# MLP on queries and routing written as one order per engine, with the last group in halves; key scaling moved to VectorE

## The chip, the cores and the metric

The kernel runs on 1 core of one Trainium2 chip. The time is that of the device in microseconds; the value to predict is the median of the runs of the changed kernel. A core has five engines with a queue each, in order: TensorE (PE, with its weight loads PEld), VectorE (DVE), ScalarE (ACT), GpSimd (POOL) and SyncE (SP, which here issues DMAs). They meet through semaphores.

## The reference, cut to what matters

Two layers, each with an attention-like part and a feed-forward part, on 8 x 512 tokens of width 128 in fp32. The change touches the second layer: test-time training (`_L1_attn_ref`) and the routing of the mixture of experts (`_L1_ffn_ref`).

```python
# x: (4096, 128)
q, k, v = split(layernorm(x) @ qkv_w + qkv_b)          # 16 heads of 8
q = q / (norm(q) + 1e-6) * qn_scale + qn_bias          # likewise k
for _ in range(2):                                     # TTT_STEPS
    grads = grad(mean(((swish(k @ gate) * (k @ val)) @ proj - v) ** 2))
    theta = {n: theta[n] - 0.1 * newton_schulz(grads[n]) for n in theta}
x = x + (swish(q @ gate) * (q @ val)) @ proj @ proj_w + proj_b
xt = layernorm(x)                                      # mixture of experts
probs = softmax(xt @ Wg + bg)                          # 8 experts, top 2
gate_vals, exp_idx = top_k(probs, 2)
pos = running count of each token within its expert    # capacity 1229
out = sum over the two experts of gelu(xt @ W1[e] + b1[e]) @ W2[e] + b2[e], weighted
```

The order of counting matters: all first choices come before all second choices.

## The kernel before

The 4096 tokens are 32 tiles of 128, in 8 groups of 4 tiles (`NG`, `G`, `W` = 512 tokens). `x` stays in SBUF throughout. The program runs in stages: the convolution of layer 0 (to about 260 us), its quantised feed-forward (to about 375), the keys (375 to 411), two steps of gradients and Newton-Schulz (411 to 931), the MLP on queries with routing (931 to 1046), scatters until 1058, and the experts.

An object `Line` chains the instructions of an engine in the order in which they are given to it (`vec`, `ten`, `act`). Where no line is used, a scheduler picks the order of the independent instructions.

**Keys** (`ttt`, stage one). For each group: `rows_of` multiplies the turned tokens by the key and value weights into PSUM (`rows`, L1159); `squares` squares on ACT (L1168) and reduces on DVE (`nrm`, L1170); DVE copies the values `v` (L1249); ACT takes the square root (L1253); `over_norm` adds, inverts and multiplies on DVE (L1175 to L1177) into `k`; PE turns `k` (`tp`, L1191); ACT scales the turned keys of the group before into `kt` (`adjusted`, L1196). ACT also copies the turned tokens two groups ahead (L1231) and normalises the group three ahead (L772). POOL applies scale and shift to `k` itself (L1262) and adds the output bias to `x` (L1265). The first gradient products (`pa`, L1489) stand behind the last turn on PE, and ACT loads a function table for the sigmoid behind them (L1493).

**MLP on queries and routing** (`ttt`, last stage, and `Moe.route`). For each group, four chunks of the hidden width: two products into PSUM (`pa` and `pb`, L1308 and L1312; four banks, so two chunks at a time), SiLU on ACT (`sw`, L1316), product on DVE (`ht`, L1317). Then `moe.route` of the group before, 16 output products (`o`, L1323) and the addition to `x` (L1327). No line is used here: the scheduler orders PE, DVE and ACT.

`route` of a group: four turns of `x` on PE (L1667) and their copy `xt`; statistics (L1672, L1673); the inverse root by three Newton steps on DVE (`rsqrt`, L87 to L95); logits on PE (L1679); normalised rows on ACT (L1686); on DVE the choice of two experts (L1692 to L1698), the copy of `hot` for the second (L1699), the row copy for the second (L1707) and running counts over the four tiles (`cum`, `seen`, L1709 to L1713); the count over tokens on PE (`pos`, L1716 and L1717); the places (L1718 to L1728, the last one writes `slot`). At last 8 indirect DMAs from POOL's queue (L1733), four for the second choice and four for the first, one for each tile. Those of the first choice wait for the second-choice DMAs of the group before. `seen` carries the counts from one group to the next.

**Experts** (`Moe.experts`). The load of the first expert's rows (`xe`, L1788, on SP) waits for every scatter. Then turn (L1817), products (L1832), Gelu on ACT (L1835, with its table load), products (L1845) and so on.

Of the kernel before, what the change touches and what calls it, by code (L numbers as in the profile page):

```python
# [1 line left out]

# [5 lines left out]
F32 = mybir.dt.float32  # L8
I32 = mybir.dt.int32
U32 = mybir.dt.uint32  # L10
AF = mybir.ActivationFunctionType
ALU = mybir.AluOpType
# [113 lines left out]
def grp(t, g):  # L126
    return t[:, g * G : (g + 1) * G, :]


def flat(ap):  # L130
    return ap.rearrange("p a b -> p (a b)")
# [780 lines left out]
def fp4_ffn(cx):  # L912
# [7 lines left out]
        "H0 G2 H1 x0 G3 P0 T0 s0 S0 A2 A3 t0 H2 H3 D0 C0 P1 S1 d0 c0 T1 U0 D1 C1 T2 C2 g0 "  # L920
        "R0 R0 W0 K0 U1 f0 O0 u0 a0 f1 f2 W1 g1 K1 W2 K2 a1 W3 E0 K3 f3 K4 K5 K6 R1 K7 R1 "
        "r0 O1 r0 o0 "
# [210 lines left out]
def ttt(cx):  # L1133
# [10 lines left out]
    with ExitStack() as st:  # L1144
# [49 lines left out]
        def adjusted(dst, tp, i):  # L1194

            return nc.scalar.activation(dst, tp, AF.Identity, bias=cols[:, i, 1:2], scale=cols[:, i, 0:1])  # L1196


        with ExitStack() as s1:
# [16 lines left out]
            FIRST, AHEAD = 4, 2  # L1216
# [8 lines left out]
            def normal(g):  # L1225
                normed[g] = xn = p2.tile([P, G, D], F32, tag="xn", name="xn", bufs=3)
                norm.act = act if g > AHEAD else free
                norm.apply(g, xn)
# [11 lines left out]
            for g in range(NG):  # L1240
# [8 lines left out]
                vec(nc.vector.tensor_copy(grp(v, g), cur[:, :, D:]))  # L1249
                if g:  # L1250
                    act(adjusted(kt[:, (g - 1) * W : g * W], tk, 1))
# [4 lines left out]
                over_norm(cur[:, :, :D], root, nrm, grp(k, g), vec)  # L1256
                if g + AHEAD + 1 < NG:
                    normal(g + AHEAD + 1)
                tk = turn(ps, "t", grp(k, g), ten)
# [33 lines left out]
        with ExitStack() as s4:  # L1293
# [10 lines left out]
            for g in range(NG):  # L1304
                ht = p2.tile([P, NF, W], F32, tag="ht", name="ht")
                for c in range(NF):
                    pa = ps_h.tile([P, W], F32, tag="h", name="pa")
                    nc.tensor.matmul(  # L1308
                        pa, gate[:, c * P : (c + 1) * P], qt[:, g * W : (g + 1) * W], start=True, stop=True
                    )  # L1310
                    pb = ps_h.tile([P, W], F32, tag="h", name="pb")
                    nc.tensor.matmul(  # L1312
                        pb, val[:, c * P : (c + 1) * P], qt[:, g * W : (g + 1) * W], start=True, stop=True
                    )
                    sw = p2.tile([P, W], F32, tag="sw", name="sw")
                    nc.scalar.activation(sw, pa, AF.Silu)  # L1316
                    nc.vector.tensor_tensor(ht[:, c, :], pb, sw, ALU.mult)  # L1317
                if g:
                    moe.route(g - 1)
                o = ps_o.tile([P, G, D], F32, tag="o", name="o")  # L1320
                for j in range(G):
                    for c in range(NF):
                        nc.tensor.matmul(  # L1323
                            o[:, j, :], ht[:, c, j * P : (j + 1) * P], w2[:, c, :],
                            start=(c == 0), stop=(c == NF - 1),
                        )
                nc.vector.tensor_tensor(grp(cx.x, g), o, grp(cx.x, g), ALU.add)  # L1327
            moe.route(NG - 1)
# [254 lines left out]

class Moe:
# [67 lines left out]

    def route(self, g):
        cx = self.cx
        nc, tc, p2 = cx.nc, cx.tc, self.p2
        vec = nc.vector

        def small(tag, *shape, dt=F32):
            return p2.tile([P, *shape], dt, tag=tag, name=tag)

        def over_e(t):
            return t.unsqueeze(2).to_broadcast([P, G, E])

        x, at = grp(cx.x, g), slice(g * G, (g + 1) * G)
        tp = self.ps_t.tile([P, G, P], F32, tag="t", name="tp")
        for j in range(G):
            nc.tensor.transpose(tp[:, j, :], x[:, j, :], cx.ident)  # L1667
        xt = small("xt", G, P)
        nc.scalar.copy(xt, tp)
        st, mv = small("st", G, 6), small("mv", G, 2)  # L1670
        for j in range(G):
            vec.bn_stats(st[:, j, :], x[:, j, :])  # L1672
            vec.bn_aggr(mv[:, j, :], st[:, j, :])  # L1673
        rs, off = small("rs", G), small("off", G)
        rsqrt(nc, p2, mv[:, :, 1], 1e-5, rs, G)
        both = self.ps_r.tile([P, 4, G, E], F32, tag="r", name="both")
        pl, pos = both[:, 3], both[:, :3]
        for j in range(G):
            nc.tensor.matmul(pl[:, j, :], xt[:, j, :], self.w_c, start=True, stop=True)  # L1679
        lg = small("lg", G, E)  # L1680
        vec.tensor_tensor(lg, pl, over_e(rs), ALU.mult)
        vec.tensor_tensor(lg, lg, self.b_g.unsqueeze(1).to_broadcast([P, G, E]), ALU.add)
        vec.scalar_tensor_tensor(off, mv[:, :, 0], -1.0, rs, ALU.mult, ALU.mult)
        rows = [self.xr[:, k, at, :] for k in range(K)]
        for j in range(G):
            nc.scalar.activation(  # L1686
                rows[0][:, j, :D], x[:, j, :], AF.Identity, bias=off[:, j : j + 1], scale=rs[:, j : j + 1]
            )

        hot, best, rk, tmp = small("hot", K + 1, G, E), small("best", K, G), small("rk", K, G), small("tmp", G, E)  # L1690
        for k in range(K):
            vec.tensor_reduce(best[:, k, :], lg, AX.X, ALU.max)  # L1692
            vec.tensor_tensor(tmp, lg, over_e(best[:, k, :]), ALU.is_equal)
            vec.tensor_tensor(tmp, tmp, self.rank, ALU.mult)
            vec.tensor_reduce(rk[:, k, :], tmp, AX.X, ALU.max)
            vec.tensor_tensor(hot[:, k], self.rank, over_e(rk[:, k, :]), ALU.is_equal)
            if k + 1 < K:
                vec.scalar_tensor_tensor(flat(lg), flat(hot[:, k]), -1e30, flat(lg), ALU.mult, ALU.add)  # L1698
        vec.tensor_copy(hot[:, K], hot[:, K - 1])  # L1699

        dif = small("dif", G)
        vec.tensor_tensor(dif, best[:, 0, :], best[:, 1, :], ALU.subtract)
        nc.scalar.activation(dif, dif, AF.Tanh, scale=0.5)
        for k, s in enumerate((0.5, -0.5)):
            vec.tensor_scalar(rows[k][:, :, D + 1], dif, s, 0.5, ALU.mult, ALU.add)

        vec.tensor_copy(rows[1][:, :, :D], rows[0][:, :, :D])  # L1707
        cum = small("cum", K + 1, G, E)
        vec.tensor_copy(cum[:, :K, 0, :], self.seen)  # L1709
        for j in range(1, G):  # L1710
            vec.tensor_tensor(cum[:, :K, j, :], cum[:, :K, j - 1, :], hot[:, :K, j - 1, :], ALU.add)
        vec.tensor_tensor(self.seen, cum[:, :K, G - 1, :], hot[:, :K, G - 1, :], ALU.add)
        vec.tensor_tensor(  # L1713
            cum[:, K], cum[:, K - 1], self.seen[:, 0:1, :].to_broadcast([P, G, E]), ALU.add
        )
        nc.tensor.matmul(pos, self.before, hot, start=True, stop=False)  # L1716
        nc.tensor.matmul(pos, self.ones, cum, start=False, stop=True)  # L1717
        vec.tensor_tensor(cum, pos, hot, ALU.mult)  # L1718
        r = small("r", K + 1, G)
        vec.tensor_reduce(r, cum, AX.X, ALU.add)  # L1720
        room = small("room", K, G)
        vec.tensor_scalar(room, r[:, ::2, :], float(CAP), None, ALU.is_lt)

        vec.tensor_scalar(r[:, 1, :], r[:, 1, :], -1.0, CAP - 1.0, ALU.mult, ALU.add)
        vec.scalar_tensor_tensor(flat(rk), flat(rk), -float(PITCH), r[:, :K, :].rearrange("p k g -> p (k g)"), ALU.mult, ALU.add)
        vec.tensor_tensor(rk, rk, room, ALU.mult)
        slot = small("slot", K, G, dt=I32)
        vec.tensor_scalar(slot, rk, float(R), None, ALU.add)  # L1728

        new = []  # L1730
        for k in (1, 0):
            for j in range(G):
                sc = nc.gpsimd.indirect_dma_start(  # L1733
                    out=self.slots.rows[:, :],
                    out_offset=bass.IndirectOffsetOnAxis(ap=slot[:, k, j : j + 1], axis=0),
                    in_=rows[k][:, j, :], in_offset=None, bounds_check=self.limit, oob_is_err=False,
                )
                tc.declare_no_dep(sc.ins, group="scatter", reason="order kept below")
                tc.add_to_no_dep_group("scatter", sc.ins)
                if k == 0 and g:  # L1740
                    self.after(sc, self.scatters[-1][:G])
                new.append(sc.ins.name)
        self.scatters.append(new)
# [178 lines left out]
```

## Time and profile before

| | us |
|---|---|
| median of 3 runs | 1241.97 (1241.28 to 1242.0) |
| profiled execution | 1242.23 |
| its span | 1240.5 |
| PE busy | 1098.0 (89%) |
| DVE busy | 754.1 (61%) |
| ACT busy | 488.5 (39%) |
| POOL busy | 736.9 (59%) |

The profiled execution is 1.7 longer than its span; what lies around the span does not show in the trace. In the views, an entry is: start, duration, engine, line of the kernel, operation, output <- inputs, and in brackets the idle time of the engine before it with what ended that. A group of matmuls (x8) counts passes: an fp32 product of two operands is two passes, a turn is one.

### The profile page before, as it was taken

What the parts mean: (1) busy time and instruction counts of PE and PEld (TensorE: products, weight loads), DVE (VectorE), ACT (ScalarE), POOL (GpSimd) and SP (SyncE); (2) the same over time, 40 slices, a digit from 0 to 9 for tenths busy, and PEclk for the clock granted to TensorE, in tenths of its full rate; (3) what the DMA queues carried; (4) which work ended last, traced back from release to release, by engine and by line L of the source; (5) the groups of instructions that cost most, each with busy time, mean ns of one, the idle gap of its engine ahead of it and who ended that gap; (6) DMA issues with size and microseconds to landing.
All of it is one profiled execution on the core that took longest, in us unless ns stands there. A gap on an engine that the chain in (4) does not pass through costs nothing.

```text
span 1240.5 us, 15616 instructions
## 1 busy us (share of the span) xinstructions
PE 1098.0 (89%) x5343; PEld 664.7 (54%) x5343; DVE 754.1 (61%) x1791; ACT 488.5 (39%) x1005; POOL 736.9 (59%) x720
## 2 busy tenths in 40 slices
PE   6899997848987799999988999999899994799983
PEld 4343442436666455555566555555576663578773
DVE  6899999988986544444455444444466785123364
ACT  4656554435657322222244232222343331243331
POOL 1356666735656888888822888888500666255552
PEclk9999999889999999999999999999999996799997
DMA  5323435960000000000000000000000111221256
GB/s 155 90 81 111 130 91 178 338 184 13 1 1 1 1 1 1 1 0 1 1 1 1 1 1 0 1 1 1 1 1 1 44 44 43 61 70 52 66 195 207
DMA packets 54606, 67.27 MB, mean 54 GB/s; under 512 B 6927, under 2 KB 32350, under 8 KB 54528
## 3 DMA queue, kind: packets, MB, share of 16 engines
q1 hardware_dynamic: 48544, 56.57, 14.7%
q0 software_dynamic: 4608, 8.43, 2.1%
q10 hardware_dynamic: 1376, 1.29, 0.3%
q8 instruction: 42, 0.69, 0.2%
q14 instruction: 36, 0.29, 0.1%
HBM read 40.00 MB, written 27.13 MB: 54 GB/s over the span
## 4 chain that ended last, share of the span: by engine, by line
PE 59%; DVE 22%; ACT 9%; issue 4%; DMA 3%; POOL 3%; ACTq 0%; DVEq 0%; POOLq 0%; SPq 0%
PE ph L1537 5%; PE po L1845 5%; PE sum L1512 5%; PE pp L1527 4%; PE ph L1832 4%; PE sum L1511 4%; PE sum L1513 4%; PE pa L1489 4%; PE pb L1491 4%; DVE v L858 3%; PE cv L492 2%; DVE pr L483 2%; PE pt L1520 2%; PE eg L357 1%; DVE ht L1317 1%
## 5 line engine op out<-in xcount | busy, mean ns | idle before, releaser
L1502 POOL TENSOR_TENSOR ds<-sw,s 128x512 f32<-128x512 f32 x64 | 81.6, 1276 | 86.3 <-DVE sw L1497 86.3
L1504 POOL TENSOR_TENSOR ds<-ds,s 128x512 f32<-128x512 f32 x64 | 111.7, 1745 | 5.0
L1733 POOL DMA_INDIRECT rows<-xr,slot x64 | 62.9, 983 | 73.8 <-DVE rs L95 45.1
L1495 ACT COPY b<-pb 128x512 f32<-128x512 f32 x64 | 37.5, 586 | 162.1 <-PE pb L1491 161.5
L1859 POOL DMA_INDIRECT res<-ye,xe x60 | 58.5, 974 | 66.9 <-DVE ye L1857 28.1
L472 POOL TENSOR_TENSOR pr<-base,en 128x512 f32<-128x512 f32 x52 | 75.0, 1473 | 36.8 <-ACT en L428 36.5
L1835 ACT ACTIVATE ht<-ph,b 128x512 f32<-128x512 f32 (+2 forms) x104 | 56.7, 576 | 94.0 <-PE ph L1832 92.7
L1499 DVE TENSOR_TENSOR h<-sw,b 128x512 f32<-128x512 f32 x64 | 50.2, 785 | 70.6 <-ACT b L1495 70.3
L483 DVE TENSOR_TENSOR pr<-base,w 128x3072 f32<-128x3072 f32 (+2 forms) x27 | 86.3, 3206 | 0.8 <-ACT w L426 0.8
L1503 POOL TENSOR_TENSOR ds<-sw,ds 128x512 f32<-128x512 f32 x64 | 82.8, 1294 | 5.0
L1505 POOL TENSOR_TENSOR ds<-ds,b 128x512 f32<-128x512 f32 x64 | 81.6, 1274 | 5.0
L1527 PEld LDWEIGHTS pp<-proj,ht 128*128 128x128 f32 x512 | 67.1, 191 | 30.7 <-issue 29.8
L1845 PE MATMUL po<-w,ht 128*128 128x128 f32 (+1 forms) x640 | 78.1, 279 | 0.0
L1522 ACT COPY ht<-pt 128x512 f32<-128x512 f32 x64 | 37.6, 587 | 101.5 <-PE pt L1520 101.5
L1832 PE MATMUL ph<-xt,w 128*128 128x512 f32 (+2 forms) x208 | 73.9, 500 | 4.0 <-DVE xt L1820 4.0
L1497 DVE TENSOR_TENSOR sw<-pa,s 128x512 f32<-128x512 f32 x64 | 44.3, 691 | 53.7 <-ACT s L1493 53.7
L1845 PEld LDWEIGHTS po<-w,ht 128*128 128x128 f32 (+1 forms) x640 | 74.9, 190 | 0.6
L1539 DVE TENSOR_TENSOR db<-ph,sw 128x512 f32<-128x512 f32 x64 | 44.2, 691 | 47.2 <-PE ph L1537 47.2
L1537 PE MATMUL ph<-proj_t,dpt 128*128 128x512 f32 x128 | 71.6, 641 | 0.0
L492 PE MATMUL cv<-pr,sel 128*32 128x512 f32 x512 | 62.3, 616 | 8.6 <-DVE pr L483 8.6
L1489 PE MATMUL pa<-gate,kt 128*128 128x512 f32 x128 | 66.8, 604 | 3.4 <-ACT b L1495 3.3
L1512 PE MATMUL sum<-db,k 128*128 128x512 f32 x128 | 66.2, 598 | 1.6 <-DVE db L1539 1.6
(359 smaller groups left out, 2548.4 us busy)
## 6 DMA issues: line engine op xcount, KB each, us to landing
base<-far SPq DMA_DIRECT2D x64, 268.0 KB, 5.2
rows<-empty SPq DMA_DIRECT2D x1, 5005.0 KB
res<-zero SPq DMA_DIRECT2D x1, 4096.0 KB, 27.1
own<-zero SPq DMA_DIRECT2D x2, 2048.0 KB, 18.8
w<-in_L_ffn_W SPq DMA_DIRECT2D x16, 256.0 KB, 4.9
y<-res SPq DMA_DIRECT2D x16, 256.0 KB, 5.5
xe<-rows SPq DMA_DIRECT2D x7, 585.0 KB, 4.3
y<-own SPq DMA_DIRECT2D x12, 256.0 KB, 5.4
```

The source lines that it names most:

```text
L483: vec(nc.vector.tensor_tensor(s["pr"][g][:, lo:hi, :], s["base"][:, lo:hi, at], w.to_broadcast([P, hi - lo, L]), ALU.mult))
L492: ten(nc.tensor.matmul(s["cv"][32 * j : 32 * (j + 1), :], sel[:, i].rearrange("p a h -> p (a h)"), s["pr"][g][:, i * NJ + j, :], start=(g ...
L1489: nc.tensor.matmul(pa, ki, gate, start=True, stop=True)
L1502: nc.gpsimd.tensor_tensor(ds, sw, s, ALU.mult)
L1503: nc.gpsimd.tensor_tensor(ds, sw, ds, ALU.subtract)
L1504: nc.gpsimd.tensor_tensor(ds, ds, s, ALU.add)
L1505: nc.gpsimd.tensor_tensor(ds, ds, b, ALU.mult)
L1512: nc.tensor.matmul(sums[1], ki, db, **kw)
L1527: nc.tensor.matmul(pp, ht[:, c * P : (c + 1) * P], proj[:, c, :], start=(c == 0), stop=(c == NF - 1))
L1537: nc.tensor.matmul(ph, dpt, proj_t, start=True, stop=True)
L1832: ten(nc.tensor.matmul(ph[:, :n], self.w1[:, e, c * P : (c + 1) * P], xt[:, :n], start=True, stop=True))
L1845: ten(nc.tensor.matmul(po[:m, i - lo, :], ht[:, c, (i - lo) * P : (i - lo) * P + m], self.w2[:, e, c, :], start=(c == 0), stop=(c == NF - ...
```

## The change

*Keys.* The scaling of the turned keys goes from ACT to DVE (all groups but the last), the value copy stands behind the key product instead of ahead of the root, and 12 products of the identity with itself stand on PE ahead of the turn of the last group.

*MLP and routing.* `Moe.route` becomes a class `Route` with the same steps as generators that put their instructions on lines. Each group runs through a table of names (`ORDER`, for the last one `LAST`): a letter for a step and a number (of a chunk, a tile or a count of instructions). `H`, `S`, `G`: hidden products, SiLU, gated product of a chunk; `O`, `x`: output products of a tile, addition; `h`, `s`: first chunk of the next group. Of the group before: `t`, `u` turn and its copy; `a` statistics; `b` roots (14 instructions); `l` logits; `c`, `d` first and second choice; `n`, `m` rows and row copy (now on ACT); `e` counts; `v` the count over tokens; `f` places and scatters. In `LAST` the capital letters T, U, A to F, L, M, N and V are the routing of the last part itself.

The last group is cut into two halves of two tiles, each with its own MLP and routing. On ACT instead of DVE: the copy of `hot`, the row copy and the gate weights. The scatters of the first choice no longer wait one by one: a small memset on POOL waits for the second-choice scatters of the group before, and they stand behind it. Behind everything ACT runs one Gelu of a single column.

```diff
+                if g:
+                    vec(nc.vector.tensor_scalar(
+                        kt[:, (g - 1) * W : g * W], tk, cols[:, 1, 0:1], cols[:, 1, 1:2], ALU.mult, ALU.add
+                    ))
-                vec(nc.vector.tensor_copy(grp(v, g), cur[:, :, D:]))
-                if g:
-                    act(adjusted(kt[:, (g - 1) * W : g * W], tk, 1))
                 root = ps_n.tile([P, G, H], F32, tag="n", name="root")
                 act(nc.scalar.activation(root, nrm, AF.Sqrt))
...
                 over_norm(cur[:, :, :D], root, nrm, grp(k, g), vec)
+                vec(nc.vector.tensor_copy(grp(v, g), cur[:, :, D:]))
...
+                if g == NG - 1:
+                    busy = ps.tile([P, W], F32, tag="t", name="busy")
+                    for _ in range(BUSY):
+                        ten(nc.tensor.matmul(busy[:, :P], cx.ident, cx.ident, start=True, stop=True))
                 tk = turn(ps, "t", grp(k, g), ten)
...
-            for g in range(NG):
-                ht = p2.tile([P, NF, W], F32, tag="ht", name="ht")
...
-                if g:
-                    moe.route(g - 1)
...
-            moe.route(NG - 1)
+            ORDER = (
+                "a2 t0 a4 H1 u0 a2 S1 l0 b1 G0 b8 H2 S2 b4 G1 b1 H3 n0 S3 n1 n2 n3 m0 c7 G2 c1 d4 G3 O0 "
+                "O1 d3 e6 v0 O2 O3 f6 x0 f2 h0 s0 "
+            )
+            LAST = (
+                "a1 H1 S1 t0 u0 a6 G0 H2 S2 a1 l0 b9 b4 G1 b1 H3 c1 S3 n0 n1 G2 c1 n2 n3 m0 G3 c2 O0 O1 "
+                "c4 d1 x0 T0 U0 d1 A1 d1 A1 d1 A2 d3 L0 e1 B1 e1 B1 e1 B1 e3 v0 B5 f1 B2 f1 B1 f1 B1 f1 "
+                "B1 f1 B1 N0 N1 C1 f1 C1 f2 C1 M0 C5 D7 E4 V0 F8 "
+            )
+            vec, ten, act = Line(tc), Line(tc), Line(tc)
+            parts = [(g * G, G) for g in range(NG - 1)] + [(NT - G, G // 2), (NT - G // 2, G // 2)]
...
+            ahead = wp.tile([P, 1], F32, tag="ahead", name="ahead")
+            act(nc.scalar.activation(ahead, cx.eps[1e-5], AF.Gelu_apprx_tanh))
...
+class Route:
...
+    def spread(self):
+        self.act(self.moe.cx.nc.scalar.copy(self.rows[1][:, :, :D], self.rows[0][:, :, :D]))
...
+    def second(self):
...
+        yield from self.choose(1)
+        self.act(nc.scalar.copy(self.hot[:, K], self.hot[:, K - 1]))
+        yield self.vec(nc.vector.tensor_tensor(dif, self.best[:, 0, :], self.best[:, 1, :], ALU.subtract))
+        self.act(nc.scalar.activation(dif, dif, AF.Tanh, scale=0.5))
+        for k, s in enumerate((0.5, -0.5)):
+            self.act(nc.scalar.activation(self.rows[k][:, :, D + 1], dif, AF.Copy, bias=0.5, scale=s))
...
+    def places(self):
...
+        for k in (1, 0):
+            if k == 0 and lo:
+                gate = nc.gpsimd.memset(self.small("gate", 1), 0.0)
+                m.after(gate, m.scatters[-1][: len(m.scatters[-1]) // K])
+            for j in range(n):
+                sc = nc.gpsimd.indirect_dma_start(
...
```

## The prediction

> **What bounds the kernel now.** The page comes first: TensorE (PE) is busy for 89% of the span, but that is an average. The windows by stage show where it is not the limit. Columns: stretch, its length, busy time of PE, weight loads, VectorE (DVE), ScalarE (ACT) and GpSimd (POOL), granted clock, DMA share, GB/s.
>
> ```profile
> 1008.00:1021.00 13.00, 12.40 (x63) 8.22 (x63) 10.25 (x59) 4.64 (x10) 7.71 (x9) 1.00 0.12 42
> 1034.00:1046.00 12.00, 4.67 (x20) 3.63 (x19) 9.43 (x66) 2.44 (x6) 7.57 (x9) 0.56 0.14 45
> 1046.00:1062.00 16.00, 0.00 (x0) 0.00 (x0) 0.00 (x0) 0.00 (x0) 9.14 (x10) 0.50 0.22 65
> ```
>
> The first is one group of the MLP on queries with routing, PE and DVE both nearly full. In the other two the last routing runs alone, then POOL alone issues scatters. The timeline there:
>
> ```profile
> 1019.89 0.68 DVE L1327 TENSOR_TENSOR x<-o,x 128x512 f32<-128x512 f32 x1
> ...
> 1033.10 0.68 DVE L1327 TENSOR_TENSOR x<-o,x 128x512 f32<-128x512 f32 x1
> ...
> 1037.16 0.17 DVE L1728 TENSOR_SCALAR slot<-rk 128x8 int32<-128x8 f32 x1 [0.24 <-DVE sq L93]
> ...
> 1037.61 0.97 POOL L1733 DMA_INDIRECT rows<-xr,slot  x1 [2.29 <-DVE rs L95]
> ...
> 1045.79 0.17 DVE L1728 TENSOR_SCALAR slot<-rk 128x8 int32<-128x8 f32 x1 [0.18 <-DVE rk L1726]
> ...
> 1056.92 0.97 POOL L1733 DMA_INDIRECT rows<-xr,slot  x1 [0.30 <-issue]
> 1059.35 0.93 SPq L1788 DMA_DIRECT2D xe<-rows  x2
> ```
>
> The slots of group 6 are there at 1037.3, 4.1 us after the add of group 7; from then POOL issues 16 scatters at 1.28 us each without a gap, and the experts' first load follows the last one's start by 2.43. The last slots (1046.0) come before POOL is free for them (1047.97). So the end of this stage is: slots of group 6, plus 16 scatters. Only an earlier start of those 16 moves it.
>
> The chain of waits at the end of the keys:
>
> ```profile
> 407.32 0.70 DVE k L1177
> 408.02 0.14 issue
> 408.15 1.09 PE tp L1191 x4
> 409.24 1.72 PE pa L1489 x2
> 410.96 0.03 ACTq L1493
> 410.99 0.03 issue
> 411.02 1.28 ACT L1493
> ```
>
> Four transposes that take 0.64 at 404.88 take 1.09 here, and a product pair that elsewhere takes 0.86 takes 1.72: the window 407.45 to 410.85 has a granted clock of 0.50, after PE had idled from 405.5 to 408.15.
>
> **Keys.** Inside the loop the period is 3.52 (square at 391.08, 394.60, 398.11). ACT alone fills it: square 0.64, key scaling 0.70, root 0.16, copy of the turn 0.48, four normalisations 1.54, start to start. Without the scaling ACT's next root must wait for DVE's reduction of the square: square 0.62, reduction 0.70, hand-over 0.02, then 0.16, 0.48, 1.54: 3.52 again. DVE's own list (0.60 reduction, 0.60 scaling, 0.24, 0.59, 0.61, 0.60 value copy) is 3.24. The loop's period gains nothing; ACT's freed time becomes a wait.
> At the head, the value copy moves behind the key product, so k of group 0 is ready 0.47 earlier (382.2 becomes 381.7) and the products `rows` of group 2 start about 0.75 earlier; they run at half clock until 387.45 now and hold the next square. I take -0.9; ends 0 and -1.2 (ACT is next late then).
> At the tail, DVE gets 0.60 more per group and the last k is ready at 407.2 instead of 407.3: -0.1. The 12 idle products are 24 passes (L1301: eight for four products) of 0.11, 2.6 us, issued after the turn of group 6 (405.5): they end at 408.1, when the last k is there; if they run late, the cost is at most 0.2. With full clock the turn saves 0.45 and the first product pair 0.86: -1.3. The last value copy now ends at 408.5 and frees the PSUM that the first product takes; that is when the turn ends, so nothing. Keys in all: **-2.3**, between -1.0 and -2.8. The gradients behind are bound by PE (445.9 of 460 us busy) and only shift.
> The Trainium skill ("TensorE: Matmul & The Clock Gate", Part 1) speaks against the idle products: it says that the clock falls after an idle window of about 3.4 us. The gap here is 2.65, and the clock fell all the same; by the rule the 1.3 would be nothing, by the row it stands.
>
> **One full group of the MLP with routing.** In the new order DVE does the routing of the group before as one chain. Cadences from rows of before (start to start): dependent operations of 128x4 0.197, of 128x32 0.2245.
>
> ```profile
> 947.17 0.16 DVE L94 TENSOR_TENSOR sq<-sq,half 128x4 f32<-128x4 f32 x1
> 947.37 0.16 DVE L95 SCALAR_TENSOR_TENSOR rs<-sq,rs 128x4 f32<-128x4 f32 x1
> 947.56 0.16 DVE L93 TENSOR_TENSOR sq<-rs 128x4 f32<-128x4 f32 x1
> 947.62 0.19 PEld L1312 LDWEIGHTS pb<-qt,val 128*128 128x128 f32 x1 [0.24 <-DVE rs L95]
> 947.64 0.69 DVE L1317 TENSOR_TENSOR ht<-pb,sw 128x512 f32<-128x512 f32 x1
> ```
>
> The next of the chain starts at 948.25: a gated product set between two links costs 0.69 - 0.20 = 0.49. From the start of one add `x`: add 0.71; statistics 1.18 (L742 to L754 at 376.10 to 377.28); 14 links of the roots 2.7; 12 links to the second `hot` 2.69; four gated products 1.96; `dif`, `cum`, `seen` 1.38 (0.22 each at 1042.40 to 1043.50). Sum 10.6. Then PE: prefix products and hand-over 0.25, output products O2 and O3 (16 passes, 0.1115 each, and 0.2 to land) 2.0. The next add starts after **12.85**. Places (1.25 us on DVE) lie beside O2 and O3; DVE waits there for about 1 us in all.
> Others: PE's list is 8 x 0.86 + 0.43 + 0.92 + 3.57 + 0.40 = 12.2, the floor. ACT gets the row copy, the hot copy and the gate weights (about 1.2 us) and sums to 6: free. Hidden H3 ends 8.0 after the add, before its gated product at 8.6; the copy of `hot` on ACT is done at 10.1, before the prefix needs it. POOL: 8 x 1.28 and one gate, a small memset (L338: 0.12), 0.3 with its hand-over: 10.5, below 12.85.
> Before, the adds are 13.03 apart (954.94 to 1033.10, six periods). The periods themselves grow from 12.7 to 13.2, which I can't explain from the lists; so the bounds are 12.4 and 13.4.
> The Trainium skill ("SBUF — State Buffer", the "DVE blocks DMA" trap) says that POOL can't write descriptors while DVE copies SBUF to SBUF in fp32. The scatters under such a row copy (L1707, 0.43) took 1.04, 1.05 and 1.11 instead of 0.97, so moving it to ACT is worth 0.1 a group on POOL by the rows, and 0.4 by the rule.
>
> **Start and halves.** The first add comes at 942.4 instead of 943.1: the 0.86 pair of group 1 no longer stands ahead of the output products (939.46 + 2.92). Six periods on, the add of group 6 is at 942.4 + 77.1 = 1019.5, where before has 1019.9: nothing gained up to here. Then the first half: its gated products are half as wide (0.37 for 128x205, L1820), so each costs 0.18, not 0.49; `cum` is done at 9.4, prefix 0.45, places 1.1, add at 10.95, slots of group 6 right behind it, POOL at 11.5: **1031.0 instead of 1037.6**, because slots come 0.3 after an add, not 4.1, and the add itself is 2 us nearer. POOL's own queue is free by then (1020.4 + 10.5 = 1030.9).
> From there: 15 x 1.28 + 3 gates of 0.3 to the last start, 1051.1, load at 1053.5 instead of 1059.35: **-5.85**. The halves must keep up: first half, 40 links of 0.1 to 0.22 with interleaving, slots 11.1 after its add (1041.5; POOL arrives at 1041.5); second half 16.3 (1046.8; POOL arrives at 1046.9). It just fits.
> **Clock in the tail.** PE idles some 2.5 us before the half-width gated product, and before fell to 0.50 at 1035.5 with such gaps. Each half-clock window adds up to 1.1 to the slots of group 6 and, over the last half (O0, O1, T, L, V at twice their time), up to 3 to the last slots. I take +1.0; ends 0 and 3.9.
> The early table load for Gelu: now 1.28 at 1066.52, but the products beside it run until 1070.5 at half clock, and PE takes up the output at 1070.9 either way. 0, at best -0.2; if those products were at full clock it would be worth 1.28.
>
> **Sum.** -2.3 - 5.85 + 1.0 = -7.15. The profiled execution took 1242.23 (span 1240.5 and 1.7 around it), 0.26 over the median of 1241.97: 1235.1 by the profile, **1234.8** as a median.
>
> **Rivals.**
> 1. *Slower: the strict chain.* DVE now waits in line at every gated product and every join; before, two routings were interleaved on it, at 0.08 to 0.12 between starts (959.59, 959.67, 959.74), which hid such waits. Each 0.1 us lost in a group is paid 7 times. From a period of 14.0 on, gain and loss cancel (7.15 / 6.5 = 1.1 over 12.85); at 14.3 the time is 1244. For it: PE's list leaves only 0.65 us of slack. Against: every producer in the list above is ready 0.5 us or more before its taker.
> 2. *Cold tail.* Both halves at half clock throughout: -1.9 instead of -4.85 in the tail; 1237.8.
> 3. *Gates stall POOL.* Each waits for the landing of scatters (2.3 to 3.6 us). If each stood 2.4 us, POOL would need 12.6 a group and be the bound from the slots of group 0 (955.9): 63 x 1.28 + 8 x 2.4 to the last start, 1055.7, -1.2 in the tail; 1238.5. Against: a gate waits for scatters of the group before, issued over 10 us earlier (5 us for the last).
> 4. *Not what it says:* the VectorE scaling frees no ACT time that counts; that is in the sum already.
>
> **Chances.** Forecast 0.58, cold tail 0.15, gates 0.07, strict chain 0.20 (a quarter of it within the limit of 0.2%, 2.5 us, which is about what a measurement tells from no change). Of the first three 0.76 end faster, 0.04 within. Faster 0.76, same 0.09, slower 0.15. Range: low end a period of 12.5, no half clock, keys at -2.8 (-2.3 - 1.0 - 0.5): 1231.0. High end 13.2 from the third group on (+2), cold tail (+2.9), keys at -1.0 (+1.3): 1241.0.
>
> **What would show it.** Adds 12.85 apart; group 6's first scatter 6.6 us earlier relative to the first add; POOL's last 16 scatters without a gap; the first product of the gradients at 0.86 a pair. A period of 13.5 or more, or a gap of POOL among the last 16, proves me wrong.

## The result, and the profile after

| | before | after |
|---|---|---|
| median of 20 runs each | 1241.53 (1240.57 to 1245.02) | 1238.89 (1235.54 to 1241.69) |
| ratio after / before | | 0.9972, 95% interval 0.9965 to 0.998 |
| profiled execution | 1242.23 (span 1240.5) | 1237.22 (span 1235.3) |
| a later set (e5), median | 1243.02 | 1237.14; ratio 0.9961, 0.9948 to 0.9974 |

By the ratios the change is faster by 3.5 us (second set: 4.8), by the medians by 2.6 (5.9), where 7.15 was forecast. The time is in the range and on the forecast side; the size is about half. The runs fell on several chips; on those of e1 to e4 and of f1 to f4 the kernel before takes 1275 us, which is told there.

The windows that were shown of before, now of after (same columns):

```profile
1008.00:1021.00 13.00, 12.48 (x70) 8.86 (x69) 10.79 (x55) 5.57 (x15) 7.88 (x9) 1.00 0.13 42
1034.00:1046.00 12.00, 5.04 (x30) 3.80 (x28) 10.64 (x73) 4.55 (x17) 8.43 (x10) 0.90 0.14 45
1046.00:1062.00 16.00, 3.81 (x10) 2.24 (x10) 1.85 (x8) 1.26 (x2) 5.94 (x7) 0.50 0.38 109
```

The full group looks as before: PE nearly full. The last routing (second line) fills DVE, and POOL is busy through it at 8.43 instead of 7.57. The timeline of after at the same place:

```profile
1019.73 0.69 DVE L1356 TENSOR_TENSOR x<-o,x 128x512 f32<-128x512 f32 x1 [0.52 <-PE o L1348]
...
1031.04 0.42 DVE L1356 TENSOR_TENSOR x<-o,x 128x256 f32<-128x256 f32 x1
1031.37 0.16 DVE L1789 TENSOR_SCALAR slot<-rk 128x8 int32<-128x8 f32 x1
...
1032.29 0.97 POOL L1797 DMA_INDIRECT rows<-xr,slot  x1 [1.01 <-DVE mv L1687]
...
1043.60 0.97 POOL L1797 DMA_INDIRECT rows<-xr,slot  x1 [1.29 <-DVE rk L1732]
...
1052.61 0.97 POOL L1797 DMA_INDIRECT rows<-xr,slot  x1 [0.30 <-DMA rows<-xr,slot]
1055.04 0.93 SPq L1922 DMA_DIRECT2D xe<-rows  x2
```

Group 6's slots come 0.33 after the first half's add, and its first scatter starts at 1032.29 instead of 1037.61. Counted from the first add that is 91.28 us where before has 94.52. The first half's scatters find POOL waiting (1.29 instead of 0.30). The load follows the last start by 2.43, as before: 4.31 earlier.

The chain of waits at the end of the keys:

```profile
404.23 0.63 PE tp L1191 x4
404.86 2.68 PE busy L1264 x24
407.54 0.05 issue
407.59 0.63 PE tp L1191 x4
408.22 1.03 PE pa L1552 x2
```

No half clock: the turn takes 0.63 (1.09 before), the first product 1.03 (1.72). The idle products hold the turn by 0.1: it starts 3.36 behind the turn before it, and 3.26 in e3, which has none.

Executions of one kernel start the keys at different times, since the code ahead, which the change leaves alone, loses clock in changing places: the first product of the keys starts at 360.97 in before's profiled execution, at 361.38 in after's, at 363.00 in e5's. The traces are therefore compared by stretches, each from one event of the timeline to the next (us):

| stretch | forecast | before | after | e5 (after again) | e6 | e7 | e8 |
|---|---|---|---|---|---|---|---|
| first product of the keys to last gradient product | -2.3 | 532.12 | 530.03 | 530.00 | 530.02 | 530.01 | 529.98 |
| to the first add | -0.7 | 50.00 | 49.60 | 49.59 | 50.86 | 49.60 | 50.86 |
| six more adds | +0.3 | 76.80 | 78.72 | 78.71 | 75.07 | 78.73 | 74.84 |
| add of group 6 to the last scatter's start | -5.4 | 37.03 | 32.88 | 32.86 | 33.49 | 32.79 | 33.41 |
| to the experts' first turn | 0 | 5.45 | 5.23 | 5.34 | 5.31 | 5.37 | 5.36 |
| to their first output product | 0 | 8.53 | 8.04 | 7.96 | 8.85 | 5.54 | 7.17 |
| to the end | 0 | 169.62 | 169.44 | 168.97 | 169.03 | 169.35 | 168.33 |
| sum | -8.1 (+1.0 for clock) | 879.55 | 873.94 | 873.43 | 872.63 | 871.39 | 869.95 |

From the keys on, after is 5.6 us shorter in this pair (6.1 with e5). The gain is in the keys (2.1), at the first add (0.4), between the add of group 6 and the last scatter (4.15) and behind it (0.9). Over the six groups between, the new lines are 1.9 us *slower* than the scheduler's order.

### The profile page after: what moved, and what is told of

Same layout as the page of the kernel before. It is cut to its first block, busy times and chain, and to the rows that moved or that the text cites. A ratio compares the mean times of both kernels' runs of the same rounds, so it can differ in the third digit from the quotient of the medians.

```text
span 1235.3 us, 15732 instructions
## 1 busy us (share of the span) xinstructions
PE 1098.2 (89%) x5387; PEld 666.7 (54%) x5387; DVE 767.0 (62%) x1808; ACT 493.4 (40%) x1041; POOL 737.2 (60%) x728
## 3 DMA queue, kind: packets, MB, share of 16 engines
q0 software_dynamic: 4608, 8.43, 2.1%
q10 hardware_dynamic: 1376, 1.29, 0.3%
## 4 chain that ended last, share of the span: by engine, by line
PE 60%; DVE 21%; ACT 9%; issue 4%; DMA 3%; POOL 3%; ACTq 0%; DVEq 0%; SPq 0%; POOLq 0%
PE ph L1600 5%; PE sum L1575 5%; PE pp L1590 4%; PE sum L1574 4%; PE sum L1576 4%; PE po L1979 4%; PE pa L1552 4%; PE ph L1966 4%; PE pb L1554 4%; DVE v L859 3%; PE cv L493 2%; DVE pr L484 2%; PE pt L1583 2%; PE o L1348 2%; DVE ht L1341 1%
```

## Experiments

**The kernel again** (e5: no edit).

> The changed kernel itself, beside before and the three variants of this set: -3.5 us against before (ratio 0.9972). In the set ahead of this one the chip gave before 1275 us and TensorE's completions reached the other engines 2 to 4.5 us late in the routing stage; if this chip does so too, the changed kernel is 20 us or more faster than before, if not, 3 to 4.

1237.14 (1235.78 to 1240.74), ratio 0.9961 (0.9948 to 0.9974). The two sets agree within their intervals, and the table shows every stretch of e5 within 0.5 us of after's. The mechanism repeats. Of the 5 us spread of single executions part lies ahead of these stretches: the two traces start the keys 1.6 us apart.

**Keys alone** (e1: before plus the keys part), **the rest alone** (e2), **no idle products** (e3).

```diff
 e1: before's queries and routing; keys as changed
 e2: -  vec(tensor_scalar(kt[g-1], tk, scale, bias))      +  act(adjusted(kt[g-1], tk, 1))
     -  12 idle products;  value copy back ahead of the scaling
 e3: -  if g == NG - 1: 12 idle products
```

> The kernel before with the keys part alone (key columns scaled by VectorE, values copied after the over-norm, twelve idle products ahead of the last turn); queries and routing as before. The forecast's sum gives -2.3 us against before (head 0.9, 0.1 at the last k, 1.3 from a warm clock). The trace of the whole change reads -1.7, since the idle products end 0.1 after the last keys and the scaling on VectorE took 0.80 us: if that reading is right, -1.7 here, between -1.3 and -2.0. If the warm clock gave nothing it would be -0.9.

> The changed kernel with the keys part of before: only queries, routing and the halved last group are new. The forecast's sum gives -4.85 us for this part. The two profiled executions read -3.3 (5.0 less 1.7), the medians of the two kernels about -1 to -1.8. If the part is worth what the sum says, -4.85; if the group period is 13.05 and not 12.85 and the last half waits for its own choices, -3.3; if most executions also lose clock in the tail that the profiled one kept, -1 to -2, with a spread of some us between executions.

> The changed kernel without the twelve idle products. TensorE is then idle for about 2.7 us ahead of the last turn of the keys. By the row of before (a gap of 2.65 us, and the turn and the first two products at half clock) it is 1.2 to 1.4 us slower than the changed kernel, with the granted clock at 0.5 for one window about 407 us. If a gap this short left the clock alone, it would be 0.1 us faster, for the idle products end 0.1 us after the keys are ready.

On their chip before took 1275.12 (1271.81 to 1277.82), e1 1273.3 (ratio 0.9988, 0.9977 to 0.9999), e2 1254.31 (0.984, 0.9823 to 0.9858), e3 1252.07 (0.9821, 0.9805 to 0.9836). The 20 us of e2 and e3 belong to the routing on this chip (below) and test none of the sums. Up to the routing the traces are those of any chip, and there they decide. The ends of the keys, timeline of PE, first e2 (keys as in before):

```profile
409.06 0.63 PE L1191 MATMUL tp<-ident,k 128*128 128x128 f32 x4 [2.65 <-DVE k L1177]
409.52 1.02 PE L1546 MATMUL pa<-gate,kt 128*128 128x512 f32 x2
410.38 1.02 PE L1548 MATMUL pb<-val,kt 128*128 128x512 f32 x2
```

then e3 (keys as changed, no idle products):

```profile
409.12 0.66 PE L1191 MATMUL tp<-ident,k 128*128 128x128 f32 x4 [2.64 <-DVE k L1177]
409.77 1.65 PE L1548 MATMUL pa<-gate,kt 128*128 128x512 f32 x2
411.21 1.92 PE L1550 MATMUL pb<-val,kt 128*128 128x512 f32 x2
```

The same gap, 2.65 and 2.64: e2 keeps the full clock, e3 loses it at 410.2. So a gap of this length costs the clock in some executions and not in others. The half clock comes and goes in steps of 3.41 us. In the step that ends with e3's loss (406.77 to 410.18) TensorE was busy for 1.06 us; in e2 the gap falls into two such steps, with 1.82 and 1.44 us busy (403.67 to 407.09 to 410.50). In e3 the loss costs 0.56 at the last gradient product (530.56 from the first product of the keys, against 530.00), not the 1.2 to 1.4 expected: the pair ends 1.4 later, but the pipeline behind it takes up most. And e2, before's keys at full clock throughout, needs 529.79, which is 0.24 *less* than the changed keys. The 2.1 us of the table are then before's two lost windows (383.5 and 407.5), not its work.

What the change does is to make such a loss less likely. With idle products ahead of the last turn, none of eleven traces loses a window there; f4 (below) is one of them, and its keys, otherwise those of before, take 530.55. Without them two of three do (before and e3, not e2). At the head, TensorE waits 2.19 us for the first turn of `k` in before's order and 1.79 in the changed one. None of the eleven traces with the changed order loses a window there; of the three with before's order two do (before, with 1.22 us busy in that window, and f4, with 1.39), and e2, with 1.67, does not. e1's keys take 530.05, and its median says -1.8 with an interval of -0.1 to -2.9, which fits; in what share of its executions before loses these windows, the runs don't show.

**The last group whole** (e4; f2 the same with the idle products of e7).

```diff
-  parts = 7 groups + two halves;  LAST interleaves both halves' routing
+  parts = 8 groups;  LAST = "ORDER, then T0 U0 A8 L0 B9 B5 N0..N3 C7 M0 C1 D7 E6 V0 F8"
```

> The changed kernel with the last group whole: eight full groups, its route alone at the end. By the rows of after its add falls at 1032.8 (1019.73 + 13.05), its slots 11.1 later at 1043.9 or, with the clock lost, 1044.9, and POOL then has eight scatters of 1.28 us and a gate ahead: last start at about 1054 to 1055 and not 1052.6. So 1.5 to 2.5 us slower than the changed kernel. If POOL's queue alone set the end, as the forecast has it (16 scatters back to back from 1032.3), halves would bring nothing: 0.

> The kernel of e7 with the last group whole. Its add falls at about 1033.0 (1019.9 + 13.1), its slots 10 to 11 us later; the eight scatters behind it start at 1044 to 1045, the last at 1053.5 to 1055 against 1052.7 of e7. So 1 to 2 us slower than e7 (ratio to before 0.9948). If POOL's queue alone sets the end, halves bring nothing, and this is within 0.5 us of e7.

Both fell on the other kind of chip. e4 took 1248.23, 3.8 *less* than e3 beside it, which differs by the halves and by the idle products (0.56). First add to last scatter is 120.90 in e4 and 124.06 in e3. f2 took 1252.45 beside 1253.65 for f3, which has the halves and lacks the early table load; first add to last scatter is 123.91 in f2 and 123.64 in f3. f2's idle products ended at 1063.02, 9.67 ahead of the turn, so its tail was cold all the same (turn 1.09, first products 6.04). There the halves are no gain, against the expectation; what they are worth where before takes 1242 us was not run, and stays open: the 4.15 of the table are read from traces, and no run on such a chip separates the halves from the new order.

**Another order of the tables** (e6).

```diff
-  a2 t0 a4 H1 u0 a2 S1 l0 b1 G0 b8 H2 S2 b4 G1 b1 H3 n0 S3 ... c7 G2 c1 d4 G3 O0 O1 d3 e6 v0 O2 O3 f6 x0 f2 h0 s0
+  H1 S1 a2 t0 u0 a6 H2 S2 b3 G1 l0 H3 b9 b2 n0 S3 ... c4 G2 h0 s0 c4 G3 O0 O1 O2 d7 e6 v0 g0 O3 f3 x0 f5
   # and: LAST without its G0; the gated product of the very first chunk ahead of all groups
```

> The changed kernel with another ORDER: the gated products 1 to 3 earlier in VectorE's line, the first hidden products of the next group ahead of the last output products, its first gated product in the wait for the prefix, and the add between the third and the fourth of the steps behind the prefix. If the period is set by VectorE's line with its two waits (0.52 and 0.62 to 0.65 us) on TensorE, both waits are filled and TensorE's own work (about 12.5 us a group) is next: a period of 12.5 against 13.05, some 3 us off the changed kernel. If the waits only move (TensorE already within 0.5 us of its own bound, with ScalarE's Silu between two products), the period stays within 0.15 of 13.05 and the time within 1 us.

The period falls to 12.51 on average (12.22 to 12.66; six adds 75.07 instead of 78.72), as the first theory says. DVE's line of after, and then of e6, at the prefix and the add:

```profile
991.87 0.26 DVE L1782 TENSOR_TENSOR cum<-pos,hot 128x96 f32<-128x96 f32 x1 [0.65 <-PE pos L1776]
993.62 0.69 DVE L1356 TENSOR_TENSOR x<-o,x 128x512 f32<-128x512 f32 x1 [0.52 <-PE o L1348]
```

```profile
991.12 0.26 DVE L1783 TENSOR_TENSOR cum<-pos,hot 128x96 f32<-128x96 f32 x1
991.98 0.69 DVE L1356 TENSOR_TENSOR x<-o,x 128x512 f32<-128x512 f32 x1
```

Both waits are gone. But the time is 1238.51 (1233.97 to 1240.85; ratio 0.9966, 0.9951 to 0.9981), no better than e5 beside it. The table says where the 3.6 us went: 1.26 back at the first add (the next group's products stand ahead of its output products), 0.6 in the last halves, 0.9 in the experts' first products, whose half clock ran longer. Only 0.8 is left from the keys on (873.43 to 872.63).

**Idle products in the tail** (e7), **and with e6's order** (e8).

```diff
-  ... E4 V0 F8
+  ... E4 W0 V0 W1 F8      # W: 16, then 44 idle products into a free bank
```

> The changed kernel with idle products on TensorE in the tail: 16 ahead of the last half's sums, 44 behind them, into a free bank. If the half clock in the tail is what costs, the last half's sums come 0.5 us earlier, the experts' first turn takes 0.6 and not 1.09 us and their first eight products 3.4 and not 5.74: 2.8 us off the profiled execution, more off the median, and a smaller spread between executions than the 6 us of the changed kernel. If the clock comes back late whatever is done (the last idle product ends some us ahead of the first expert's rows), nothing: within 0.5 us.

> The order of e6 and the idle products of e7 together. If they act on different stretches the gains add: about 6 us off the changed kernel. If POOL's queue of scatters is next once the slots come earlier (eight scatters a group take 10.5 us, so it isn't within a period of 12.5), the sum falls short by what POOL waits less.

e7: 1235.86 (1234.9 to 1236.34), ratio 0.9948 (0.9935 to 0.9961); the spread is 1.4 us where e5 has 5.0. PE's timeline of after at the experts' start, and then of e7:

```profile
1057.84 1.09 PE L1951 MATMUL tp<-ident,xe 128*128 128x128 f32 x4 [11.25 <-DMA xe<-rows]
1059.86 5.74 PE L1966 MATMUL ph<-xt,w 128*128 128x512 f32 x8 [0.94 <-DVE xt L1954]
```

```profile
1046.38 10.06 PE L1378 MATMUL busy<-ident 128*128 128x128 f32 x88
1058.10 0.63 PE L1956 MATMUL tp<-ident,xe 128*128 128x128 f32 x4 [1.67 <-DMA xe<-rows]
1059.67 3.70 PE L1971 MATMUL ph<-xt,w 128*128 128x512 f32 x8 [0.94 <-DVE xt L1959]
```

The stretch falls from 8.04 to 5.54; all others stay within 0.15. By the medians e7 is only 1.3 under e5 beside it. The sums of the last half are read 0.24 us sooner behind their input (0.5 was expected), but the last scatter does not move (32.79 against 32.88), because POOL is the later of the two there. e8: 1234.63 (1233.31 to 1235.2), ratio 0.9938 (0.9925 to 0.9951), the best of all runs: 2.5 under e5's median beside it, 8.4 under before's. From the keys on e8 is 3.48 shorter than e5, where e6 alone has 0.80 and e7 alone 2.04: the gains add, but not to the 6 that was expected. The late first add and the slower halves of e6 stay, and the tail gave less than in e7: e8's idle products ended at 1054.2, 1.7 us ahead of the turn as in e7, but here the clock fell for one window at 1057.3, and the first products took 5.33. TensorE was busy for 0.91 us in the 3.41 ahead of that, where e7's last idle products ran until 1056.4 and its windows (1053.97 to 1060.80) have 2.47 and 1.76.

**Mending e8** (f1: the first group in the old order of products, the first half in after's order, 50 idle products, four more behind the first turn), **the price of the early table load** (f3: e7 without `ahead`), **before with idle products alone** (f4).

```diff
 f1: +  {0: START, 1: SECOND, NG - 1: HALF, NG: LAST}.get(i, ORDER)    W: 16, 50;  4 behind the first turn
 f3: -  act(activation(ahead, eps, Gelu))
 f4: before + 12 idle products ahead of the last turn of the keys, 62 behind the last sums
```

> The order of e6, with the first group in the old order of products (its add came 1.26 us late in e6), the first half in the changed kernel's own order, and idle products in the tail as in e7, six more of them, and four behind the experts' first turn. By the rows of e8: the first add back to 941.2 from 942.3, the period 12.5, no half clock in the experts' first products (5.33 to 3.7 us). So 2 to 3 us under e8 (ratio to before 0.9938), near 1232, with a spread of 2 us. If the first interval only gives back what the first add gains, 1 to 1.5 us under e8, from the clock alone.

> The kernel of e7 without the early activation that brings in Gelu's table. The load (1.28 us) then stands ahead of the experts' first Gelu. With the clock at full the eight first products take 3.7 us and the four Gelus behind the load end 0.4 to 1.3 us later: that much slower than e7. If the load still fits beside the products, as at half clock in before, 0.

> The kernel before, with its schedule as it was, and idle products in two places: the twelve ahead of the last turn of the keys, and 62 behind the last group's sums, up to the experts' first turn. If the clock alone explains much of the change, this is 3 to 5 us faster than before: 0.5 to 2 in the keys (before loses the clock there in some executions and in others not) and 2.5 to 3 at the experts' first products. Then the lines of queries and routing are worth the rest of e7's 6 us, 1 to 3. If the clock matters little, within 1 us of before.

All three fell on a chip of the other kind (before 1275.15, 1271.6 to 1278.54), so their times say nothing on e8: f1 1254.07 (ratio 0.9833), f3 1253.65 (0.9834), f4 1275.69 (1.0008, 0.9996 to 1.002). What their traces show: f1's first add is back at 49.60 and its experts' first stretch at 5.54, both as meant. But on that chip the idle products end late, at 1077.2 in f1 and 1076.0 in f3, and hold up the experts' first turn: from the last scatter to it are 7.08 and 7.78, where e3 has 5.48. Of the 2.65 that the first products gain on e3's 8.19, that gives back 1.6 and 2.3. Whether f1 beats e8 where before takes 1242 us is open. f4 gains nothing as a whole. Its keys are 1.57 shorter than before's (530.55 against 532.12), but its other idle products do not stand where they were meant to. No line holds them: they run from 1058.3 on, and 72 of their 124 passes stand ahead of the last sums. The last prefix is read 5.2 us behind its products, POOL waits 3.68 for the slots, and the last scatter starts 46.66 behind the add of group 6, where e1 has 42.82. They ended at 1086.5, 9.3 us ahead of a turn that came at 1095.77 here, so the tail was cold again. What the clock alone is worth in the tail of before stays open. f3 shows the table load, timeline of ACT:

```profile
1079.08 1.28 ACT L1972 ACT_TABLE_LOAD   x1 [17.39 <-PE ph L1969]
1080.37 2.42 ACT L1972 ACTIVATE ht<-ph,b 128x512 f32<-128x512 f32 x4
```

In e7 the Gelus wait for their products; here they run back to back behind the load and catch up with PE. The output products start 5.54 behind the turn in both and take 4.23 instead of 3.74: at full clock the preload is worth 0.5.

## Why the prediction was half right

By its own steps, in the frame of the table; the forecast said -7.15, the pair of profiled executions measured -5.6, and the medians -2.6 (ratio: -3.5). Of its own signs of being wrong one came true, the gap of POOL among its last 16 scatters, and the period is over 12.85 though not at 13.5; the first scatter of group 6 is 3.2 us earlier relative to the first add, not 6.6 (by the forecast's own times, 942.4 and 1031.0, it would be 5.9).

- *Keys, -2.3:* measured -2.1 in the pair, and that it is so near is luck: the price was read off an execution of before that had lost two windows, as part of its schedule. e2, with before's keys and no loss, leaves nothing to gain. "The loop's period gains nothing" came out: squares are 3.51 to 3.52 apart in after (383.20 to 397.27), as in e2. The -0.9 at the head is the lost window at 383.5: the turn of group 6's keys starts 43.91 behind the first product of the keys in before, 42.85 in after, 42.84 in e2. At the tail DVE is slower than assumed: the scaling takes 0.72 from start to start and not 0.60, DVE is busy for 16.38 of 17.00 us (387 to 404), and the last two turns come 3.44 and 3.36 apart, in e2 3.28 and 3.27.
- *First add, -0.7:* -0.4; the 26 passes behind the last gated product take 3.17 until the last one ends, not 2.92.
- *Period 12.85:* 13.12 over the six. Between the adds at 993.62 and 1006.67 the chain to the end of `cum` takes 10.68 (forecast 10.6), the prefix's round on PE to O2 0.36 (0.25), O2 and O3 with their landing 2.01 (2.0): 13.05. Two of the six are longer: 13.34, where a gated product waits on PE (0.24 at 987.63), which the list gave 0.5 us of room, and 13.19, from small delays along the chain. This is the mis-sized term, +1.6 over six groups. e6 takes O2 out of that path and reaches 12.51, so the chain made the period, not PE's list.
- *Halves:* the first add 11.31 behind that of group 6 instead of 10.95 (+0.4); the scatter starts 0.92 behind its slots, not 0.25 (+0.7; the profile names the aggregate behind the slots in DVE's line, `mv`, as what released it); from there to the last start 20.32, forecast 20.1. "POOL's last 16 without a gap" was wrong: it stands 1.0 longer ahead of the first half's. The gates cost 0.1 or nothing and not 0.3, which hides most of that. Together +1.3.
- *Clock in the tail, +1.0:* nothing at the slots. The clock fell at 1043.5, after the first half's prefix; the second half's sums are slow (0.66 each), but POOL, still at the first half's scatters, is the later one. It costs at the experts' first products instead, 2.5 us by e7's trace, and before pays that as well (8.53), so it isn't a part of the difference. "0" for the early table load was right at half clock: in before and e1, which load the table there, the output products take 3.74 as in after.
- Sum of the misses: +1.6 +1.3 +0.3 +0.2 -1.0, and -0.9 behind the scatters, is +1.5: the pair. The 2 to 3 us from there to the medians are executions: after's profiled one lies 1.7 under its median, before's 0.7 over, and before's had the two lost windows.
- *Rivals:* the strict chain was the right direction (1.9 us slower over the groups), at a quarter of the price that would have turned the sign (0.27 of 1.1 a group). The cold tail had the right cause in the wrong place. The gates stand nowhere: 0.12, then 0.26 to the next start, no landing waited for.

The Trainium skill ("TensorE: Matmul & The Clock Gate", Part 1) says that the window of about 3.4 us is free-running. That agrees: the half-clock stretches in all traces last 3.4 us or multiples (6.8, 10.2, 20.5; only the end of the program cuts one). Its rule that an idle window is needed does not hold here: e3's gap is 2.64 long, shorter than a window. What the traces show is how long TensorE was busy in a window. In all fourteen, a window at full clock with less than 1.4 of its 3.41 us busy is followed by half clock (0.63 and 1.22 in before, 1.06 in e3, 0.91 in e8), and one with more than 1.95 never is; between the two both occur (1.44 is kept in e2, 1.73 is not in e6 at 1036.6). By this a gap of 2.65 is kept or lost with the place at which the windows cut it.

## What to carry over

A lost clock in a profile is a property of the execution until a second trace shows it; compare stretches between two traces, from an event behind the code that changes, before pricing it. When a chain crosses to another engine and back, take the whole round from a row (0.36 here, 0.65 back to VectorE), not the length of the two instructions. Idle products in a stretch where TensorE waits anyway bought 2.5 us in one profiled execution, 1.3 by the medians, and a spread of 1.4 us instead of 5 (five and six executions). Their number is tuned to one timing: where the stretch shifted, they ended too early (f2, f4) or held up the work behind them (f1, f3).

## What the runs showed of the hardware

On the chips of e1 to e4 and of f1 to f4 before takes 1275 us in every execution (1271.6 to 1278.5), elsewhere 1240.6 to 1245. Up to the first add their traces agree with the others; in the routing the other engines go on late behind TensorE's products. An add of before in e1, and the prefix's reading in e2, each after its engine had been idle:

```profile
987.13 0.69 DVE L1333 TENSOR_TENSOR x<-o,x 128x512 f32<-128x512 f32 x1 [4.50 <-remote]
```

```profile
1026.76 0.26 DVE L1776 TENSOR_TENSOR cum<-pos,hot 128x96 f32<-128x96 f32 x1 [2.64 <-PE o L1342]
```

In e1 the add of the last five groups starts 4.1 to 5.1 us behind the last output product (0.4 to 0.6 in before where it takes 1242), and SiLU behind its own product as late, both released within 0.1 us. In e2 the prefix is read 2.1 us behind its products (0.11 in after), when the next 16 output passes have ended. At the last prefix of e1, with nothing behind it on TensorE, the reading is not late; in f4, with idle products behind it, it is, by 5.2 us. The last sums of f3 have idle products behind them too and are read within 0.1, so work behind is not all of it. The new order loses less to this: the six adds take 85.33 in e2 and 101.91 in e1, which is 16.6 of the 20 us there. What holds the other engines back, no run here tells; it is the largest number of the study, and open.
